# Projection's first product of blocks 2 to 28 made of seven 128x128 products, with half a tile lowered on VectorE and two row statistics on ScalarE

## The chip, the cores and the metric

The kernel runs on one core of a Trainium2 chip. The metric is the device time of one execution in microseconds. The kernel before took 998.61 us, the median of three runs (997.31 to 998.91).

Five engines work side by side, each through its own queue and in the order of that queue: TensorE (PE; its weight loads are shown apart as PEld), VectorE (DVE), ScalarE (ACT), GpSimd (POOL) and SyncE (SP), which issues the transfers. They wait for each other by semaphores.

## The reference

A cross attention with an adaptive layer norm in front and a residual behind, all in float32. With 16 sequences of 1024 rows (`x`) and of 64 context rows, width 512 and 16 heads of width 32:

```python
def _ada_ln(x, c, W_ss, b_ss):
    h = (x - mean(x)) / sqrt(var(x) + 1e-5)
    scale, bias = split(silu(c) @ W_ss + b_ss, 2)
    return (1 + scale)[:, None, :] * h + bias[:, None, :]

xq  = _ada_ln(x,   cond, Wss_q,  bss_q)        # (16, 1024, 512)
xkv = _ada_ln(ctx, cond, Wss_kv, bss_kv)       # (16,   64, 512)
q = (xq @ Wq + bq)                             # 16 heads of 32
k, v = split(xkv @ Wkv + bkv)
attn = softmax(q @ k.T / sqrt(32))             # over 64 context rows
return x + (attn @ v) @ Wp + bp
```

## The kernel before

The 16,384 rows of `x` are worked off in 32 blocks of 512 rows (`NB` = 32, `TB` = 512), four row tiles of 128 each. A block passes through: load, row statistics (`q_stats`, VectorE: L287 and L288 for each row tile; `q_scale` makes 1/sqrt(var) of them in small steps on ScalarE and GpSimd), normalising (`hidden`, ScalarE, L344), a transposition (`turn` on VectorE and `move` by transfers), scale and shift (`scale_features`, ScalarE, L459), the query product, the scores (`score_products`, L755, small tiles of 32x32), the softmax, the product with the values (`mix`, L1002 or L1013, small tiles), the projection, the addition of the residual (`added`, VectorE, L1288) and the store.

Softmax: the maximum over the context rows is taken on VectorE from PSUM (`maximum`, L772; `maxima`, L801 spreads it, tile `mb`), ScalarE copies the scores from PSUM to memory (`copied`, L781, half a tile each, 128x1024), GpSimd subtracts the maximum (`subtract`, L814, 128x2048; two tiles, `s_tiles[i, 0]` and `s_tiles[i, 1]`, for a block), ScalarE takes the exponential (`weights`, L836), GpSimd adds the two tiles up (`total`, L902).

Both large products of a block are 512x512x512, and both are made by Strassen's way: seven products of half the size instead of eight, with sums of features and of weights ahead and sums of results behind. They are numbered 1 to 7 and made in the order that buffers allow. One such product is four matmuls of 128x128 weights by 128x256 features, two records each in the trace. For the query product, L551 are the plain products, and products 1 and 7 are taken apart once more: `quarter_products` (L622) makes each of seven products of 128x128, the first four, then three. For this GpSimd prepares sums of features (`feature_quarters`, L598 to L600) in `t_quarters`, ScalarE copies two intermediate results there (`quarter_copies`, L633), and VectorE makes three additions (`quarter_adds`, L639 to L641). `feature_sums` (L510, GpSimd) are the sums of the outer level.

The projection's outer level is `product(i, n)` (L1155), with the attention's result `ot`, weights `w_p_sb` or their sums `WT`, and PSUM banks `pp`, two for a block. `row_sum` (L1120 to L1127, GpSimd) are its sums of rows; `biased` (L1099, ScalarE) seeds a bank with the bias, and `output_seed` (L1108) copies the result of product 1 into the second bank, where product 2 is added. Products 1, 6, 5 and 3 go to the one bank, 2, 7 and 4 to the other. In before all seven are plain.

What an engine does next is not decided by a scheduler: the calls stand in an order written out by hand, and each engine takes its instructions in that order. Blocks 0 to 2 and the last ones are written out call by call; a loop between them (`for i in range(3, NB - 2)`) works on several blocks in each turn: scores of block `i`, projection of blocks `i - 1` and `i - 2`, query product of block `i + 1`, normalising of blocks `i + 3` and `i + 4`. Several functions that the changed order calls stand in the file before as well and are not called there, or for a few blocks only: `q_stats_two`, `q_square_mean`, `lowered`, `subtract_half` and the `inner_...` functions.

Of the kernel before, what the change touches and what calls it, by code (L numbers as in the profile page):

```python
# [15 lines left out]
P = 128  # L16
# [4 lines left out]
def cross_attention_block(  # L21
# [1587 lines left out]
    load_residual(0)  # L1609
    feature_sums(2, nc.gpsimd, (3,))  # L1610
    subtract(1, zs=(0,))
    q_stats(5, (0,))
    subtract(1, zs=(1,))
    value_move('B', (3,))
    q_stats(5, (1,))
    query_product(2, 2)
    q_stats(5, (2,))
    scale_features(3, (0,))
    turn(4, (0,))
    scale_features(3, (3,))  # L1620
    context_product('B', 'v', 3)
    load_residual(1)
    query_out(2, 2)
    value_move('B', (2,))
    query_product(2, 6)
    context_out('B', 'v', 3)
    hidden(4, (1,))
    scale_features(3, (2,))
    weights(1, 0)
    query_product(2, 7)  # L1630
    spread_rows(0)
    divided(0)
    query_out(2, 6)
    value_move('B', (1,))
    query_product(2, 5)
    value_move('B', (0,))
    query_out(2, 7)
    query_product(2, 4)
    query_added(2, 5)
    query_product(2, 3)  # L1640
    feature_sums(3, nc.gpsimd, (0,))
    turn(4, (1,))
    row_sums(0, 0)
    weights(1, 1)
    total(1)
    swapped(1)
    biased(0, 2)
    query_added(2, 4)
    feature_sums(3, nc.gpsimd, (1,))
    query_out(2, 3)  # L1650
    q_stats(5, (3,))
    hidden(4, (3,))
    q_scale(5)
    turn(4, (2,))
    product(0, 1)
    added(0, 1)
# [402 lines left out]
```

## Time and profile before

| What | Value |
|---|---|
| median of three runs | 998.61 us (997.31 to 998.91) |
| profiled execution, its time | 996.79 us |
| profiled execution, its span | 994.9 us |
| granted TensorE clock | 1.00 |
| TensorE busy | 982.9 us, 99% |
| VectorE busy | 898.5 us, 90% |
| GpSimd busy | 893.0 us, 90% |
| ScalarE busy | 780.2 us, 78% |
| one turn of the loop | 28.52 us |

The span runs from the first to the last instruction of the profiled execution; its time has 1.9 us more around it. In rows of the groups, the first number behind the bar is the time that the group was busy, the second the mean of one instruction in ns; behind the second bar stands the idle time of the engine just before them. In rows of the timeline the first number is the start, the second the duration, and xN says how many records one row holds; what stands in brackets is a wait and what ended it.

### The profile page before, as it was taken

Reading aid. Unit: us, or ns where it says so; the run is one execution under the profiler, and the core shown is the slowest. Engines: PE = TensorE matmul, PEld = TensorE weight load, DVE = VectorE, ACT = ScalarE, POOL = GpSimd, SP = SyncE. Lnnn points to the kernel's source line nnn. Section 1 sums busy time; section 2 is a strip of 40 time slices with the busy share of each in tenths; the row PEclk is TensorE's granted clock in tenths of the full one; section 3 lists DMA queues with packets and bytes.
Section 4 is the critical chain, followed back from the end, with each engine's and each line's share of the span. In section 5 each row is a group of like instructions: output and inputs, shape, how many; then the busy total and the mean of one; then the engine's idle time right before and its main releaser. Section 6 shows DMA issues by size and latency. Waiting matters only on the chain.

```text
span 994.9 us, 20661 instructions
## 1 busy us (share of the span) xinstructions
PE 982.9 (99%) x7501; PEld 767.7 (77%) x7501; DVE 898.5 (90%) x1326; ACT 780.2 (78%) x1169; POOL 893.0 (90%) x695
## 2 busy tenths in 40 slices
PE   8999999999999999999999999999999999999997
PEld 7888777777777777777777778777787787777776
DVE  7687899999999999999999999999999999987995
ACT  3878868888888888888888888888888888876540
POOL 2687999999999999999999999999999999999861
PEclk9999999999999999999999999999999999999999
DMA  9765755555656555556655555565555556544323
GB/s 316 257 173 148 172 161 143 156 161 171 190 181 181 164 152 164 142 180 191 184 178 159 160 154 151 182 188 181 178 152 172 149 155 182 148 135 131 116 90 108
DMA packets 114885, 165.52 MB, mean 166 GB/s; under 512 B 34872, under 2 KB 46160, under 8 KB 112864
## 3 DMA queue, kind: packets, MB, share of 16 engines
q1 hardware_dynamic: 114400, 163.67, 55.2%
q8 instruction: 60, 0.98, 0.4%
q0 software_dynamic: 384, 0.54, 0.2%
q14 instruction: 41, 0.34, 0.1%
HBM read 79.21 MB, written 34.60 MB: 114 GB/s over the span
## 4 chain that ended last, share of the span: by engine, by line
PE 94%; POOL 1%; DMA 1%; SPq 1%; DVE 1%; issue 1%; DVEq 0%; ACT 0%; POOLq 0%
PE pp L1155 37%; PE pq L551 29%; PE pq L622 10%; PE ps L755 7%; PE po L1002 6%; PE pk_A L551 1%; PE pv_B L551 1%; PE pk_B L551 1%; PE pv_A L551 1%; DMA w_k_sb<-in_L_xcond_Wkv_dram 1%; PE pp_0b L1155 1%; POOL sum L902 0%; SPq L166 0%; SPq L143 0%; DVE m L772 0%
## 5 line engine op out<-in xcount | busy, mean ns | idle before, releaser
L814 POOL TENSOR_TENSOR s<-s,mb 128x2048 f32<-128x2048 f32 x63 | 286.1, 4563 | 16.5 <-DVE mb L801 9.2
L1155 PE MATMUL pp<-w_p_sb,ot 128*128 128x256 f32 x756 | 178.9, 380 | 0.2 <-DVE ot L981 0.2
L772 DVE TRANSPOSE_TENSOR_REDUCE m<-ps 128x32 f32<-128x1024 f32 x128 | 152.3, 1226 | 10.0 <-PE ps L755 9.7
L781 ACT COPY s<-ps 128x1024 f32<-128x1024 f32 x126 | 127.4, 1013 | 41.8 <-PE ps L755 36.9
L1155 PEld LDWEIGHTS pp<-w_p_sb,ot 128*128 128x128 f32 x756 | 141.2, 190 | 21.9 <-issue 1.9
L662 ACT ACTIVATE qt<-pq,bias_t 128x256 f32<-128x256 f32 x256 | 107.5, 474 | 52.9 <-PE pq L622 27.8
L902 POOL TENSOR_TENSOR sum<-s,p 128x2048 f32<-128x2048 f32 x30 | 136.4, 4547 | 1.6 <-ACT p L836 1.6
L1288 DVE TENSOR_TENSOR r<-pp,r 128x512 f32<-128x512 f32 x188 | 123.6, 669 | 14.2 <-ACT xt L459 6.8
L551 PE MATMUL pq<-xt,w_q_sums 128*128 128x256 f32 x512 | 123.8, 385 | 0.0
L1155 PE MATMUL pp<-WT,ot 128*128 128x256 f32 x508 | 122.0, 383 | 0.0
L551 PEld LDWEIGHTS pq<-xt,w_q_sums 128*128 128x128 f32 x512 | 95.2, 190 | 34.3 <-issue 22.6
L1155 PE MATMUL pp<-WT,s 128*128 128x256 f32 x504 | 119.6, 380 | 0.7 <-DVE r L1288 0.5
L861 ACT ACTIVATE s<-s 32x2048 f32<-32x2048 f32 x60 | 114.6, 1910 | 1.5
L1155 PEld LDWEIGHTS pp<-WT,ot 128*128 128x128 f32 x508 | 94.2, 190 | 17.8 <-issue 3.0
L1155 PEld LDWEIGHTS pp<-WT,s 128*128 128x128 f32 x504 | 91.5, 191 | 11.9 <-DVE r L1288 1.4
L344 ACT ACTIVATE x<-x,rstdq 128x512 f32<-128x512 f32 x128 | 94.8, 807 | 1.0 <-POOL rstdq L305 0.9
L459 ACT ACTIVATE xt<-xt,ss_q 128x512 f32<-128x512 f32 x124 | 93.9, 807 | 0.5 <-DMA xt<-ht 0.3
L981 DVE TENSOR_TENSOR ot<-po,vb 128x1024 f32<-128x1024 f32 x64 | 75.5, 1219 | 18.8 <-PE po L1002 17.4
L287 DVE BATCH_NORM_STATS2 bs<-x 128x6 f32<-128x512 f32 x128 | 85.3, 666 | 0.0
L510 POOL TENSOR_TENSOR xt_sums<-xt 128x512 f32<-128x512 f32 x64 | 81.2, 1268 | 1.4 <-ACT xt L459 0.9
L374 DVE STREAM_TRANSPOSE ht<-x 128x512 f32<-128x512 f32 x124 | 77.7, 679 | 4.3 <-ACT x L344 2.2
L907 DVE TRANSPOSE_TENSOR_REDUCE lt<-sum 128x64 f32<-128x2048 f32 x31 | 71.6, 2310 | 6.2 <-POOL sum L902 3.9
(221 smaller groups left out, 1957.6 us busy)
## 6 DMA issues: line engine op xcount, KB each, us to landing
x<-in_x_dram SPq DMA_DIRECT2D x32, 1024.0 KB, 5.4
r<-in_x_dram SPq DMA_DIRECT2D x32, 1024.0 KB, 5.7
out_dram<-r SPq DMA_DIRECT2D x62, 512.0 KB, 5.0
xt<-ht SPq DMA_DIRECT2D x488, 64.0 KB, 2.0
p<-s SPq DMA_DIRECT2D x60, 256.0 KB, 3.8
wss_kv<-in_L_xcond_Wss_kv_dram SPq DMA_DIRECT2D x4, 512.0 KB, 7.2
wss_q<-in_L_xcond_Wss_q_dram SPq DMA_DIRECT2D x4, 512.0 KB, 10.5
vr<-ltd SPq DMA_DIRECT2D x128, 8.0 KB, 1.8
```

Source lines behind the costliest of these rows:

```text
L344: nc.scalar.activation(dst, src, AF.Identity, bias=rstd[:, 1, j : j + 1], scale=rstd[:, 0, j : j + 1])
L459: nc.scalar.activation(xt[:, :, c, :], xt[:, :, c, :], AF.Identity, scale=ss["q"][:, c, b : b + 1], bias=ss["q"][:, NC + c, b : b + 1],)
L551: nc.tensor.matmul(out_, lhsT=lhsT, rhs=rhs, start=new and m == 0 and c == 0, stop=c == HC - 1, skip_group_check=True,)
L622: nc.tensor.matmul(qa["q", k][:, q * P : (q + 1) * P], lhsT=lhsT, rhs=rhs, start=first and q == 0, stop=True, skip_group_check=True,)
L662: nc.scalar.activation(dst, src, AF.Identity, bias=bq_t[:, o : o + 1])
L772: nc.vector.tensor_reduce(m_tiles[i][:, z, 2 * e : 2 * e + 2, :], s_banks[i, z][e].rearrange("p r (j a) -> p r j a", a=32), AX.X, ALU.max, ...
L781: nc.scalar.copy(s_tiles[i, z][:, 2 * e : 2 * e + 2, :], s_banks[i, z][e])
L814: eng.tensor_tensor(s_tiles[i, z], s_tiles[i, z], mb_tiles[i], ALU.subtract)
L861: nc.scalar.activation(s_tiles[i, 0][at + 32 : at + 64], raw_tiles[i][at : at + 32], AF.Exp, scale=SCALE)
L902: nc.gpsimd.tensor_tensor(t, s_tiles[i, 0], s_tiles[i, 1], ALU.add)
L1155: nc.tensor.matmul(to, lhsT=rows[:, c, t * P : (t + 1) * P], rhs=cols[:, c, :], start=n == 2 and (i, 2) not in seeded and t == 0 and c == ...
L1288: nc.vector.tensor_add(r, a, r)
```

## The change

Four things change together.

1. The projection's product 1 of blocks 2 to 28 is made of seven 128x128 products (`inner_products`, TensorE, L1246, four and then three), as products 1 and 7 of the query already are. With it come for each of these blocks: `inner_quarters` (GpSimd, L1223 to L1225), `inner_biased` (two ScalarE copies of 128x256, L1205 and L1206, instead of one of 128x512, L1099), `inner_copies` (ScalarE, L1257) and `inner_adds` (VectorE, L1263 to L1265). `inner_weight_sums(1)` (six sums on GpSimd, L1188 to L1195) runs once. One of its results is written over a 128x128 piece of `w_p_sb`, which is loaded again (64 KB) before the plain product 1 of block 30.
2. In these blocks one half of the second score tile is lowered by its maximum on VectorE straight from PSUM (`lowered(i, 0)`, L818) instead of being copied by ScalarE and lowered by GpSimd; GpSimd does the other half only (`subtract_half`, L825, 128x1024, instead of L814 with 128x2048).
3. The statistics of row tiles 0 and 1 of blocks 7 to 31 are made on ScalarE (`q_stats_two`: two activations with an accumulated output each, L331 and L332) with one small GpSimd instruction (`q_square_mean`, L337), instead of L287 and L288 on VectorE.
4. The order from `mix(0)` on is rewritten. In the turn of block `i` products 3 and 4 are now of block `i - 3` and the mix and the first products of block `i - 2`, so the projection lags further behind; the loop runs over 5 to 27, and blocks 28 to 31 are written out.

Instructions, before and after: L1155 884 to 776 matmuls of 128x256, L1246 0 to 189 of 128x128; L287 and L288 136 to 86 each; L818 2 to 29; L781 126 to 99; L814 63 to 36; L825 0 to 27.

The diff, cut to its core (in the loop the conditions that always hold are left out):

```diff
@@ load_projection
         if again:
-            nc.sync.dma_start(w_p_sb[:, : NC // 2, :], src[:, : NC // 2, :])
+            nc.sync.dma_start(w_p_sb[:, 0, P : 2 * P], src[:, 0, P : 2 * P])
@@ head, blocks 2 and 3
...
+    subtract(3, zs=(0,))
+    lowered(3, 0)
...
+    mix(2)
+    subtract_half(3, 1, 1)
...
+    inner_weight_sums(1)
+    query_product(4, 5)
+    feature_quarters(5, 1)
+    query_out(4, 7)
+    divided(2, (0,))
+    inner_quarters(2, 1)
+    turn(6, (3,))
+    inner_biased(2, 1)
+    q_stats_two(7, (0,))
+    q_stats_two(7, (1,))
...
@@ the loop
-    for i in range(3, NB - 2):
+    for i in range(5, NB - 4):
...
+            lowered(a, 0)
+            product(i - 3, 3)
+            product(i - 3, 4)
+            subtract(a, zs=(0,))
...
+            mix(b)
...
+            inner_biased(b, 1)
+            weights(a, 0)
+            quarter_products(i, 7, False)
+            subtract_half(a, 1, 1)
...
+            inner_quarters(b, 1)
+            query_out(i, 7)
+            total(a)
+            turn(f, (2,))
+            q_stats_two(i + 3, (0,))
+            inner_products(b, 1, True)
+            inner_copies(b, 1)
+            query_added(i, 5)
+            turn(f, (3,))
+            load_x(i + 4)
+            inner_adds(b, 1)
+            query_product(i, 4)
+            query_product(i, 3)
+            query_added(i, 4)
+            move(f, ks=(0,))
+            q_stats_two(i + 3, (1,))
+            row_sum(b, 0)
+            inner_products(b, 1, False)
...
+            output_seed(b)
...
@@ block 30, near the end
+    load_projection(again=True)
+    query_product(z, 3)
...
+    product(y - 1, 1)
```

The functions of the inner product, which both files hold:

```python
def inner_products(i, v, first):
    w, s = (lambda m, c: inner_weight(v, m, c)), (lambda k: inner_sum(v, k))
    t, x = inner_tiles[i, v], inner_rows(i, v)
    if first:
        todo = ((0, w(0, 0), x[:, 0, 0, :]), (2, s(0), t[:, 0]),
                (1, s(2), t[:, 1]), (3, s(1), t[:, 2]))
    else:
        todo = ((0, w(0, 1), x[:, 0, 1, :]), (2, s(3), x[:, 1, 1, :]), (1, w(1, 1), t[:, 3]))
    for q, rhs, lhsT in todo:
        nc.tensor.matmul(acc[acc_bank(i, v)][:, q * P : (q + 1) * P], lhsT=lhsT, rhs=rhs, ...)

def inner_adds(i, v):
    a, t, tt = acc[acc_bank(i, v)], inner_tiles[i, v], nc.vector.tensor_tensor
    both_ = a[:, P : 3 * P].rearrange("p (k n) -> p k n", k=2)
    tt(t[:, 2], a[:, 3 * P :], t[:, 0], ALU.add)
    tt(both_, both_, t[:, 2:3].to_broadcast([P, 2, P]), ALU.add)
    tt(a[:, 3 * P :], a[:, P : 2 * P], t[:, 1], ALU.add)
```

TensorE's queue in a turn of the loop, between the mix and the next scores. L551 and L622 are the query, `pp` the projection; in before:

```order
L551 MATMUL pq_1_3746<-xt_3385,w_q_sums 128x256 x4
L1155 MATMUL pp_2_3890<-w_p_sb,ot_3879 128x256 x4
L551 MATMUL pq_7_3816<-xt_sums,w_q_sb 128x256 x4
L1155 MATMUL pp_2_3904<-w_p_sb,ot_3879 128x256 x4
L551 MATMUL pq_1_3746<-xt_3385,w_q_sums 128x256 x4
L1155 MATMUL pp_3_3953<-WT,ot_3879 128x256 x4
```

The same place in after:

```order
L551 MATMUL pq_1_5498<-xt_5171,w_q_sums 128x256 x4
L1246 MATMUL pp_2_5676<-w_p_sb,ot_5697 128x128
L1246 MATMUL pp_2_5676<-first_sums,first_5701 128x128
L1246 MATMUL pp_2_5676<-w_p_sb,first_5701 128x128
L1246 MATMUL pp_2_5676<-first_sums,first_5701 128x128
L551 MATMUL pq_7_5628<-xt_sums,w_q_sb 128x256 x4
L551 MATMUL pq_1_5498<-xt_5171,w_q_sums 128x256 x4
L1246 MATMUL pp_2_5676<-w_p_sb,ot_5697 128x128
L1246 MATMUL pp_2_5676<-first_sums,ot_5697 128x128
L1246 MATMUL pp_2_5676<-w_p_sb,first_5701 128x128
```

The four matmuls of product 1 became seven small ones around two query products, and products 2 and 7 of the block moved behind the scores.

GpSimd's queue at the entry of the loop, behind the query's weight sums, in before (`s`, `mb`: scores and maxima; `t_quarters`, `xt_sums`: features of the query; L1120, L1122 and L1125: sums of rows for the projection):

```order
L814 TENSOR_TENSOR s_0_1584<-s_0_1584,mb_1641 128x2048
L814 TENSOR_TENSOR s_1_1617<-s_1_1617,mb_1641 128x2048
L1120 TENSOR_TENSOR s_2_1725<-ot_1719 128x512
L1122 TENSOR_TENSOR ot_1719<-ot_1719 128x2x256
L902 TENSOR_TENSOR sum_1755<-s_0_1584,p_1742 128x2048
L1125 TENSOR_TENSOR s_2_1774<-ot_1719,s_2_1725 128x512
```

And in after, for the same block's subtraction:

```order
L814 TENSOR_TENSOR s_0_1527<-s_0_1527,mb_1637 128x2048
L825 TENSOR_TENSOR s_1_1594<-s_1_1594,mb_1637 128x1024
L1188 TENSOR_TENSOR first_sums<-w_p_sb 128x128
L1189 TENSOR_TENSOR first_sums<-first_sums,w_p_sb 128x128
L1190 TENSOR_TENSOR w_p_sb<-w_p_sb 128x128
L1191 TENSOR_TENSOR first_sums<-w_p_sb,first_sums 128x128
L1194 COPY first_bias<-b_p_sb 128x128
L1195 TENSOR_TENSOR first_bias<-b_p_sb 128x128
L598 TENSOR_TENSOR t_quarters<-xt_1497 128x256
L599 TENSOR_TENSOR t_quarters<-xt_1497,t_quarters 128x128
L600 TENSOR_TENSOR t_quarters<-xt_1497,t_quarters 128x128
L1223 TENSOR_TENSOR first_1734<-ot_1732 128x256
```

The second subtraction is half as wide, the weight sums and the sums of both kinds stand ahead of the sums of rows and of the row total L902.

ScalarE's queue in the loop around the seed of product 1, in before (L836: exponentials, L662: the query's result, L459: scale and shift):

```order
L1099 COPY pp_2_6050<-b_p_sb 128x512
L836 ACTIVATE s_0_5904<-s_0_5904 128x2048
L836 ACTIVATE p_6062<-s_1_5937 128x2048
L1108 COPY pp_2_6064<-pp_2_6050 128x512
L459 ACTIVATE xt_5815<-xt_5815,ss_q 128x4x128 x3
L1099 COPY pp_3_6113<-b_diff 128x512
```

And in after:

```order
L1205 COPY pp_2_5676<-first_bias 128x256
L1206 COPY pp_2_5676<-zero 128x256
L836 ACTIVATE s_0_5497<-s_0_5497 128x2048
L836 ACTIVATE p_5691<-s_1_5586 128x2048
L662 ACTIVATE qt_5604<-pq_7_5628,bias_t 128x2x4x32 x2
L331 ACTIVATE squares_0_5711,mvq_5710<-x_5439 128x512
L332 ACTIVATE squares_0_5711,mvq_5710<-x_5439,mvq_5710 128x512
L1257 COPY first_5701<-pp_2_5676 128x256
L331 ACTIVATE squares_1_5742,mvq_5710<-x_5439 128x512
L332 ACTIVATE squares_1_5742,mvq_5710<-x_5439,mvq_5710 128x512
```

Between the exponentials and the seed of product 2 there now stand the query's result, four statistics and the inner copy, which TensorE's last three small matmuls need by way of VectorE.

More of the change, by code (lines that the diff above doesn't have):

```diff
@@ new lines, in cross_attention_block @@
+    added(1, 4)
+    inner_products(2, 1, True)
+    quarter_products(5, 1, True)
+    inner_copies(2, 1)
+    q_stats(7, (2,))
+    move(6, ks=(0,))
+    q_stats(7, (3,))
+    total(3)
+    move(6, ks=(1,))
+    quarter_copies(5, 1)
+    query_added(4, 4)
+    scale_features(5, (2,))
+    score_products(4, 0)
+    copied(4, 0, 1)
+    inner_adds(2, 1)
+    inner_products(2, 1, False)
+    output_seed(2)
+    row_sum(2, 2)
+    swapped(3)
+    quarter_adds(5, 1)
+    move(6, ks=(2,))
+    scale_features(5, (3,))
@@ L1787, in cross_attention_block @@
[L1787 to L1803 removed]
+        if i >= 4:
+            biased(b, 3)
@@ new lines, in cross_attention_block @@
+    subtract(27, zs=(0,))
+    lowered(27, 0)
+    quarter_products(28, 7, True)
+    turn(30, (0,))
+    query_out(28, 6)
+    scale_features(29, (0,))
+    product(25, 3)
+    scale_features(29, (1,))
+    quarter_copies(28, 7)
+    spread_rows(26)
+    product(25, 4)
+    quarter_adds(28, 7)
+    hidden(30, (2,))
+    mix(26)
+    turn(30, (1,))
+    added(25, 3)
+    scale_features(29, (3,))
+    subtract_half(27, 1, 1)
+    divided(26, (0,))
+    weights(27, 0)
+    quarter_products(28, 7, False)
@@ new lines, in cross_attention_block @@
+    divided(26, (1,))
+    feature_quarters(29, 1)
+    turn(30, (2,))
+    q_stats_two(31, (0,))
+    inner_biased(26, 1)
+    query_out(28, 7)
+    weights(27, 1)
+    turn(30, (3,))
+    query_product(28, 5)
+    inner_quarters(26, 1)
+    inner_products(26, 1, True)
+    query_product(28, 4)
+    added(25, 4)
+    query_added(28, 5)
+    inner_copies(26, 1)
+    query_product(28, 3)
+    inner_adds(26, 1)
+    inner_products(26, 1, False)
+    q_stats_two(31, (1,))
+    move(30, ks=(0,))
+    query_added(28, 4)
@@ new lines, in cross_attention_block @@
+    hidden(31, (3,))
+    turn(31, (0,))
+    added(26, 3)
+    scale_features(30, (2,))
+    query_out(29, 7)
+    row_sum(26, 3)
+    turn(31, (1,))
+    product(26, 4)
+    turn(31, (2,))
+    spread_rows(27)
+    mix(27)
+    query_added(29, 5)
+    query_product(29, 3)
+    load_residual(27)
+    inner_biased(27, 1)
+    divided(27, (0,))
+    subtract(28, zs=(0,))
+    turn(31, (3,))
+    added(26, 4)
+    subtract_half(28, 1, 1)
+    scale_features(30, (3,))
+    feature_sums(30, nc.gpsimd, (0,))
@@ new lines, in cross_attention_block @@
+    weights(28, 0)
+    move(31, ks=(0,))
+    move(31, ks=(1,))
+    move(31, ks=(2,))
+    query_product(29, 4)
+    feature_quarters(30, 1)
+    feature_sums(30, nc.gpsimd, (1,))
+    inner_quarters(27, 1)
+    weights(28, 1)
+    inner_products(27, 1, True)
+    query_out(29, 3)
+    divided(27, (1,))
+    total(28)
+    query_added(29, 4)
+    inner_copies(27, 1)
+    quarter_products(30, 1, True)
+    quarter_copies(30, 1)
+    inner_adds(27, 1)
+    swapped(28)
+    score_products(29, 0)
@@ new lines, in cross_attention_block @@
+    scale_features(31, (0,))
+    product(27, 4)
+    subtract(29, zs=(0,))
+    weights(29, 0)
+    added(27, 5)
+    product(27, 3)
+    lowered(29, 0)
+    load_residual(NB - 1)
+    spread_rows(28)
+    mix(28)
+    quarter_adds(30, 7)
+    added(27, 3)
+    divided(28, (0,))
+    quarter_products(30, 7, False)
+    subtract_half(29, 1, 1)
+    inner_quarters(28, 1)
+    query_product(30, 5)
+    inner_biased(28, 1)
+    query_out(30, 7)
+    added(27, 4)
+    weights(29, 1)
+    inner_products(28, 1, True)
```

829 lines of the change are left out of this document (543 added, 286 removed).

## The prediction

> **What bounds the kernel now.** I read the page first: busy shares, then the chain that ended last.
>
> ```profile
> span 994.9 us, 20661 instructions
> PE 982.9 (99%) x7501; PEld 767.7 (77%) x7501; DVE 898.5 (90%) x1326; ACT 780.2 (78%) x1169; POOL 893.0 (90%) x695
> PE 94%; POOL 1%; DMA 1%; SPq 1%; DVE 1%; issue 1%; DVEq 0%; ACT 0%; POOLq 0%
> ```
>
> TensorE is busy 982.9 of 994.9 us and the chain lies on it for 94%; VectorE and GpSimd follow at 90%. The waits of TensorE agree (total, times, longest): beside the start of the program none is above 0.6 us. Below them stands one of four windows, each one turn of the loop (28.52 us between equal instructions), and the mean of the four; the columns are PE, PEld, DVE, ACT, POOL.
>
> ```profile
> PE pc L210 <- DMA early<-in_cond_dram: 2.7, 1, 2.7
> PE ps L755 <- ACT qt L662: 0.6, 1, 0.6
> ```
>
> ```profile
> 478.25:506.77 28.52, 28.52 (x221) 22.20 (x220) 26.96 (x40) 24.02 (x36) 27.51 (x22) 1.00 0.57 170
> ...
> sum 114.08, PE 114.08 PEld 88.77 DVE 108.01 ACT 96.03 POOL 110.11; mean PE 28.52 PEld 22.19 DVE 27.00 ACT 24.01 POOL 27.53
> ```
>
> In the loop TensorE never idles, at granted clock 1.00. So only less TensorE work shortens a turn, and only while VectorE (27.00), GpSimd (27.53) and ScalarE (24.01) stay below the new period and hand over in time.
>
> **TensorE's part.** The timeline of TensorE gives the price of both kinds of product, start to start (x counts two records per matmul).
>
> ```profile
> 502.66 0.38 PE L622 MATMUL pq<-xt_sums,w_q_sums 128*128 128x128 f32 x2
> 502.88 0.83 PE L622 MATMUL pq<-t_quarters,w_p_sb 128*128 128x128 f32 x6
> 503.55 1.89 PE L1155 MATMUL pp<-w_p_sb,ot 128*128 128x256 f32 x8
> 505.28 1.89 PE L1155 MATMUL pp<-WT,ot 128*128 128x256 f32 x8
> ...
> 518.38 1.96 PE L1155 MATMUL pp<-WT,ot 128*128 128x256 f32 x8
> 520.26 1.14 PE L755 MATMUL ps<-qt,K_B 32*32 32x512 f32 x32
> 521.33 0.49 PE L622 MATMUL pq<-xt,w_q_sb 128*128 128x128 f32 x2
> ```
>
> A plain product (8 records 128x256) holds TensorE 505.28 − 503.55 = 1.73 us. Eight records 128x128 take 503.55 − 502.66 = 0.89, or 0.111 each; the nested product has seven matmuls, 14 records, 1.56. Saved: 0.165 per block, and for blocks 2 to 28, 27 of them, **4.5 us**. The new period would be 28.36. A change between full and small tiles costs about 0.15 (518.38 + 1.73 = 520.11, but the scores start at 520.26); the built program has 200 such changes in both kernels, so nothing is added there.
>
> The rows weigh against a rule of the Trainium skill ("TensorE: Matmul & The Clock Gate", section "Back-to-back issue gap"): in a stream of weight load and matmul pairs, spacing is set by both, about 81 ns a matmul at N=128 and 131 at N=512. By that rule halving N would not halve the time. It is rival D below; here 0.111 against 0.216 is a half.
>
> ```profile
> L622 PEld LDWEIGHTS pq<-t_quarters,w_q_sb 128*128 128x128 f32 x224 | 29.5, 192 | 0.0
> ```
>
> A weight load lasts 192 ns by its record, yet records follow each other every 111 ns, so loads overlap among themselves.
>
> **VectorE.** Rows from the groups of instructions.
>
> ```profile
> L818 DVE TENSOR_TENSOR s<-ps,mb 128x1024 f32<-128x1024 f32 x2 | 2.4, 1220 | 0.1
> L287 DVE BATCH_NORM_STATS2 bs<-x 128x6 f32<-128x512 f32 x128 | 85.3, 666 | 0.0
> L288 DVE BATCH_NORM_AGGREGATE mvq<-bs 128x2 f32<-128x6 f32 x128 | 23.3, 182 | 4.4
> L639 DVE TENSOR_TENSOR t_quarters<-pq,t_quarters 128x128 f32<-128x128 f32 x56 | 15.0, 267 | 2.1 <-ACT t_quarters L633 2.1
> L640 DVE TENSOR_TENSOR pq<-pq,t_quarters 128x256 f32<-128x256 f32 x56 | 24.2, 433 | 1.9
> L641 DVE TENSOR_TENSOR pq<-pq,t_quarters 128x128 f32<-128x128 f32 x56 | 16.8, 299 | 1.9
> ```
>
> Per turn it gains one `lowered` (1.22) and three inner additions of the shapes of L639 to L641 (0.27 + 0.43 + 0.30 = 1.00), and loses two statistics pairs (2 x 0.85 = 1.70): 27.00 + 0.52 = 27.5 of 28.36. Still covered, with 0.8 us to spare instead of 1.5.
>
> **ScalarE.**
>
> ```profile
> L781 ACT COPY s<-ps 128x1024 f32<-128x1024 f32 x126 | 127.4, 1013 | 41.8 <-PE ps L755 36.9 <-DVE m L772 3.9
> L344 ACT ACTIVATE x<-x,rstdq 128x512 f32<-128x512 f32 x128 | 94.8, 807 | 1.0 <-POOL rstdq L305 0.9
> L297 ACT ACTIVATE workq<-workq,ln_half 128x4 f32<-128x4 f32 x34 | 10.1, 297 | 1.1
> L1099 ACT COPY pp<-b_p_sb 128x512 f32<-128x512 f32 x31 | 18.4, 593 | 0.2 <-DVE r L1288 0.2
> L633 ACT COPY t_quarters<-pq 128x256 f32<-128x256 f32 x56 | 21.0, 374 | 2.7 <-PE pq L622 1.8
> ```
>
> It loses one copy (1.01) and gains an inner copy (0.37), two seed copies of 256 for one of 512 (2 x 0.37 − 0.59 = 0.15), and four statistics. No statistic with an accumulated output is in this trace. Lower end: a plain copy of 512 without one, 0.59. Upper end: L344 plus a whole small instruction for writing the accumulator, 0.81 + 0.30 = 1.11. I take 0.81, an activation of the same size from memory to memory. Sum: 24.01 − 1.01 + 0.37 + 0.15 + 3.24 = **26.8** (25.9 to 28.0), below 28.36 even at the upper end, but there with hardly any slack; it becomes the bound from 1.21 per statistic on.
>
> The Trainium skill ("ScalarE: Activation LUTs", section "What ACT_TABLE_LOAD costs") gives 186 ns plus 0.833 ns per element, and 93 more per pointer operand; from that an estimate is 0.61 for the mean and 0.71 for the square, which would make the sum 26.2. L344 has two such operands, where the page's estimate is 0.80 and the trace has 0.807.
>
> **GpSimd.** Its timeline in the first turns, start to start:
>
> ```profile
> 100.76 9.09 POOL L814 TENSOR_TENSOR s<-s,mb 128x2048 f32<-128x2048 f32 x2 [3.52 <-DVE mb L801]
> ...
> 186.90 0.74 POOL L598 TENSOR_TENSOR t_quarters<-xt_sums 128x256 f32<-128x256 f32 x1
> 187.72 0.46 POOL L599 TENSOR_TENSOR t_quarters<-xt_sums,t_quarters 128x128 f32<-128x128 f32 x1
> 188.26 0.45 POOL L600 TENSOR_TENSOR t_quarters<-xt_sums,t_quarters 128x128 f32<-128x128 f32 x1
> 188.67 9.08 POOL L814 TENSOR_TENSOR s<-s,mb 128x2048 f32<-128x2048 f32 x2
> 197.71 1.29 POOL L1120 TENSOR_TENSOR s<-ot 128x512 f32<-128x512 f32 x1
> 199.08 1.28 POOL L1122 TENSOR_TENSOR ot<-ot 128x512 f32<-128x512 f32 x1
> 200.61 4.54 POOL L902 TENSOR_TENSOR sum<-s,p 128x2048 f32<-128x2048 f32 x1 [0.25 <-ACT p L836]
> ...
> 217.15 9.08 POOL L814 TENSOR_TENSOR s<-s,mb 128x2048 f32<-128x2048 f32 x2
> ```
>
> From 188.67 to 217.15 are 28.48 us with one wait of 0.25: 28.2 of work per turn. A full subtraction costs (197.71 − 188.67)/2 = 4.52. Half of one is not in the trace: at the least a 128x512 one (1.28), at the most the full one (4.52); by the straight line through the two sizes 2.36, which I take. Three quarter sums take 188.67 − 186.90 = 1.77. The mean of squares is tiny, 0.1 to 0.45 (L600 is larger); I take 0.3. Sum: 28.2 − 4.52 + 2.36 + 1.77 + 0.3 = **28.1** of 28.36 (27.0 to 30.3). GpSimd stays as tight as before: 0.25 us of slack per turn.
>
> **The entry of the loop** is where that hurts. GpSimd works through from 100.76 on in before; the window that begins there says the same, 103.41 us of busy time in 105.84:
>
> ```profile
> 100.69:206.53 105.84, 105.56 (x761) 81.72 (x760) 95.60 (x137) 85.38 (x126) 103.41 (x72) 1.00 0.60 168
> ...
> 100.69 1.09 PE L1002 MATMUL po<-s,V_A 64*32 64x512 f32 x16
> ```
>
> The changed order starts from the same place (`mix(0)` on TensorE at 100.69, the subtraction of block 1 on GpSimd at 100.76). From there I counted each queue up to the first inner product of block 3, the second turn that has one. GpSimd, through the second of its three inner sums: nine full subtractions and row totals (40.7), two halves (4.7), 28 sums of 128x512 at 1.26 (35.3), three sets of small statistics (3.0), five sets of quarter sums (8.9), the quarter sums of query weights (1.8), the six new weight sums of 128x128 at about 0.45 (2.7), the inner sums (3.1) and one mean (0.3): 100.5, so ready at 201.2. TensorE up to there: 168 matmuls of 128x256 (72.6), 38 of 128x128 (8.5), 160 small ones of scores and mix (13.9), 19 tile changes (2.8): 97.8, so wanted at 198.5. TensorE comes early because the projection of older blocks has been pushed behind this point, and GpSimd comes late because of the weight sums. It has to stand still about **2.7 us** in blocks 1 to 3. With the half subtraction at its ends, this stall is 0.6 or 7.0. It is paid once: afterwards GpSimd (28.1) is the faster of the two.
>
> Other edits: the reload of a 64 KB piece of the weights is one more DMA on SP's queue, with the third query product and the scores of block 31 as cover (1.73 and about 1.07, from the starts above); 0.5 to 1 us of exposure if that cover is gone. In the tail TensorE waits 0.6 and less four times before; the new tail has three projection products less of the last block but one behind it and the same dependence on the row maxima, so I leave it at zero, plus or minus 0.5. For hand-overs inside the loop that are just missed I put 0.4 in all.
>
> **Sum**: −4.5 + 2.7 + 0.4 = −1.4 us of the 994.9 span, 993.5; the profiled execution was 996.79, the median of the runs 998.61, so I shift by 3.7 and get **997.2**.
>
> **Rivals.**
> A. The stall at the entry does not appear, since other engines let TensorE fall behind there anyway, or GpSimd's work fits its waits: then the whole saving stays, 998.6 − 4.4 = 994.2. For it: in before GpSimd is no less loaded and TensorE loses 0.28 of 105.84 there. Against: the count. Chance 0.23.
> B. Slower: the inner product's second half becomes a wait in every turn. TensorE issues four inner matmuls, two query products (3.46 us), and then three inner matmuls that need `inner_adds`; these stand in VectorE's queue behind a transposition and a query addition, and need `inner_copies`, which stands in ScalarE's queue behind the first two statistics. Worked out: up to 1.62 for the statistics already begun, 0.37 copy, 1.00 additions, about 0.7 for what VectorE has begun: 3.7 against 3.46. It decides from 0.05 us per turn on (27 x 0.05 = 1.4, the forecast gain). At 0.2 it costs 5.4, so 1002.6; at the upper price of a statistic (2.2 for the two) 0.8 a turn, 1019. For it: four engines at 95 to 99% of the period. Against: in before GpSimd at 28.2 of 28.52 costs nothing. Chance 0.20.
> C. The half subtraction costs nearly a full one: a stall of 7.0 at the entry, net +2.9, 1001.5, and GpSimd's 30.3 would then bound the loop, +1.9 x 25 more. For a price near the line speak both sizes. Chance 0.10, mostly near 1001.
> D. The 128-wide pieces pay for their weight loads: 14 x 0.192 = 2.69 against 1.73, +0.96 x 27 = 26 us, 1024. The starts of L622 speak against it. Chance 0.02.
>
> **Numbers.** The forecast (own range 995.5 to 998.9) has 0.45. A change of 0.2%, 2 us, is about what a measurement of this kernel tells from none. Faster: A, and a quarter of the forecast, 0.35. Slower: most of B, half of C, and D, 0.23. Same: the rest, 0.42. Range: A's 994.2 less 0.2 below; above up to B's first case, 1002.
>
> **What would show it.** Right: L1246 with 128x128 records 0.111 apart; a loop period of 28.36 with TensorE at 100%; waits of TensorE for GpSimd's `pp`, `s` or `first` in about 170 to 200 us, 2 to 3 us in all; L331 and L332 near 0.8; L825 near 2.36. Wrong: a period of 28.5 or more with waits on VectorE at L1246 (B), L825 near 4.5 (C), L1246 0.19 apart (D), or no waits before 210 us (A).

## The result, and the profile after

The changed kernel takes 1060.95 us (median of four runs, 1056.81 to 1062.59) against 998.35 for the kernel before (four runs of its own): a ratio of 1.062, with a 95% interval of 1.059 to 1.066. It is 62.6 us slower. Forecast were 997.2 us and a range of 994 to 1002. The profiled execution took 1056.81 us, its span is 1055.0, against 994.9.

The page of the changed kernel, its busy shares and its chain:

```profile
span 1055.0 us, 21526 instructions
PE 1003.3 (95%) x7663; PEld 783.9 (74%) x7663; DVE 914.0 (87%) x1334; ACT 834.3 (79%) x1396; POOL 885.8 (84%) x807
PE 45%; DMA 17%; DVE 14%; SPq 12%; issue 8%; POOL 2%; ACT 2%; DVEq 0%; POOLq 0%; ACTq 0%
PE pq L551 14%; PE pp L1155 13%; SPq L399 9%; DMA x<-in_x_dram 6%; DMA ltd<-lt 4%; DMA vr<-ltd 4%; PE ps L755 4%; DVE r L1288 4%; PE pq L622 3%; PE pp L1246 3%; DVE ot L981 3%; DVE ht L374 3%; SPq L927 2%; DVE m L772 1%; PE po L1002 1%
```

No engine took TensorE's place as the bound: PE has 95%, the others less. What came into the chain is SyncE's queue and transfers, 29% of the span together (DMA 17%, SPq 12%), where before had 2%. `L399` is `move`, `ltd` and `vr` are the row sums of the softmax on their way through memory (`inverse_rows`: one store, L925, and four loads, L927). One turn of the loop, columns as before (PE, PEld, DVE, ACT, POOL):

```profile
485.15:515.90 30.75, 29.27 (x228) 22.79 (x227) 27.41 (x40) 26.32 (x45) 27.14 (x26) 1.00 0.50 150
```

Waits by total, number and longest, of all engines and of SyncE's queue:

```profile
ACT pp L1205 <- DVE r L1288: 62.6, 24, 3.7
DVE vb L957 <- DMA vr<-ltd: 60.3, 25, 4.4
...
PE pq L622 <- DVE pq L641: 30.7, 20, 4.1
PE pp L1246 <- POOL first L1223: 3.6, 20, 0.2
```

```profile
SPq L399 <- PE pq L551: 43.9, 26, 2.4
...
SPq L399 <- DMA x<-in_x_dram: 38.0, 18, 5.1
```

VectorE stands 60.3 us, 2.4 in each of 25 blocks, ahead of `spread_rows` (L957), for the row sums. In its queue behind that stand an addition of the residual, for which ScalarE's seed of product 1 (L1205) waits, and the query's additions, for which TensorE waits. Where the row sums are, SyncE's timeline shows. One turn in before:

```profile
486.10 0.38 SPq L119 DMA_DIRECT2D x<-in_x_dram  x1
489.86 1.15 SPq L841 DMA_DIRECT2D p<-s  x2
491.10 9.01 SPq L399 DMA_DIRECT2D xt<-ht  x12
500.21 0.53 SPq L925 DMA_DIRECT2D ltd<-lt  x1
501.89 1.75 SPq L927 DMA_DIRECT2D vr<-ltd  x4
503.98 2.41 SPq L399 DMA_DIRECT2D xt<-ht  x4
```

And in after, with VectorE's wait for the row sums of the turn ahead and one piece of the chain of work:

```profile
515.88 0.38 SPq L119 DMA_DIRECT2D x<-in_x_dram  x1
517.92 2.44 SPq L399 DMA_DIRECT2D xt<-ht  x4
520.40 1.25 SPq L841 DMA_DIRECT2D p<-s  x2
521.69 12.62 SPq L399 DMA_DIRECT2D xt<-ht  x12
534.42 0.52 SPq L925 DMA_DIRECT2D ltd<-lt  x1
```

```profile
506.01 2.31 DVE L957 STREAM_TRANSPOSE vb<-vr 128x2048 f32<-128x2048 f32 x1 [2.53 <-DMA vr<-ltd]
...
524.64 0.51 DVE L922 RECIPROCAL lt<-lt 128x64 f32<-128x64 f32 x1
```

```profile
515.88 10.44 DMA x<-in_x_dram
...
526.33 0.51 SPq L399
```

The reciprocals of the row sums are done at 525.1, but their store is issued at 534.42, behind twelve `move`s. One of these waited until 526.33, when the 1 MB load of `x` had landed after 10.44 us. The program gives the transfers of a queue eight semaphores in turn, so that each waits for the one eight places ahead of it; the sixth `move` stands eight places behind the load, and both have the same semaphore in the trace. (The turn shown is the longest of the 23, 33.57 us; in the one ahead of it the twelve `move`s take 10.33.) In before, the twelve moves start 5.0 us behind the load, the row sums are issued 14.1 us behind it and not 18.5, and VectorE asks for them later.

From start to start of `spread_rows`, the loop takes (907.8 − 200.3)/23 = 30.76 us a turn, against (847.9 − 192.8)/23 = 28.48. Up to block 3's `spread_rows` the kernel is 7.5 us late (200.30 against 192.78), in the 23 turns behind it loses 52.4, and in the rest 0.2: 60.1, all of 1055.0 − 994.9.

### The profile page after: what moved, and what is told of

Same layout as the page of the kernel before. It is cut to its first block, busy times and chain, and to the rows that moved or that the text cites. A ratio compares the mean times of both kernels' runs of the same rounds, so it can differ in the third digit from the quotient of the medians.

```text
span 1055.0 us, 21526 instructions
## 1 busy us (share of the span) xinstructions
PE 1003.3 (95%) x7663; PEld 783.9 (74%) x7663; DVE 914.0 (87%) x1334; ACT 834.3 (79%) x1396; POOL 885.8 (84%) x807
## 4 chain that ended last, share of the span: by engine, by line
PE 45%; DMA 17%; DVE 14%; SPq 12%; issue 8%; POOL 2%; ACT 2%; DVEq 0%; POOLq 0%; ACTq 0%
PE pq L551 14%; PE pp L1155 13%; SPq L399 9%; DMA x<-in_x_dram 6%; DMA ltd<-lt 4%; DMA vr<-ltd 4%; PE ps L755 4%; DVE r L1288 4%; PE pq L622 3%; PE pp L1246 3%; DVE ot L981 3%; DVE ht L374 3%; SPq L927 2%; DVE m L772 1%; PE po L1002 1%
## 5 line engine op out<-in xcount | busy, mean ns | idle before, releaser
L814 POOL TENSOR_TENSOR s<-s,mb 128x2048 f32<-128x2048 f32 x36 | 163.8, 4554 | 11.4 <-DVE mb L801 7.5
L902 POOL TENSOR_TENSOR sum<-s,p 128x2048 f32<-128x2048 f32 x30 | 136.5, 4549 | 1.3 <-ACT p L836 1.3
L662 ACT ACTIVATE qt<-pq,bias_t 128x256 f32<-128x256 f32 x256 | 106.2, 466 | 35.6 <-PE pq L551 33.0
L1155 PE MATMUL pp<-w_p_sb,ot 128*128 128x256 f32 x540 | 127.9, 380 | 0.6 <-DVE ot L981 0.5
L551 PE MATMUL pq<-xt,w_q_sums 128*128 128x256 f32 x512 | 123.9, 386 | 2.6 <-ACT qt L662 1.8
L957 DVE STREAM_TRANSPOSE vb<-vr 128x2048 f32<-128x2048 f32 (+1 forms) x33 | 74.0, 2242 | 60.3 <-DMA vr<-ltd 60.3
L1155 PE MATMUL pp<-WT,ot 128*128 128x256 f32 x508 | 120.2, 380 | 0.5 <-ACT pp L1099 0.5
L1155 PE MATMUL pp<-WT,s 128*128 128x256 f32 x504 | 119.4, 379 | 1.1 <-DVE r L1288 1.1
L1155 PEld LDWEIGHTS pp<-w_p_sb,ot 128*128 128x128 f32 x540 | 100.0, 190 | 16.0 <-issue 1.7
L551 PEld LDWEIGHTS pq<-xt,w_q_sums 128*128 128x128 f32 x512 | 96.6, 194 | 17.6 <-DVE qt L669 3.2
L344 ACT ACTIVATE x<-x,rstdq 128x512 f32<-128x512 f32 x128 | 102.8, 814 | 5.4 <-POOL rstdq L305 4.4
L781 ACT COPY s<-ps 128x1024 f32<-128x1024 f32 x99 | 98.7, 999 | 10.6 <-PE ps L755 5.8
L1155 PEld LDWEIGHTS pp<-WT,s 128*128 128x128 f32 x504 | 95.4, 190 | 15.2 <-DVE r L1288 1.5
L1155 PEld LDWEIGHTS pp<-WT,ot 128*128 128x128 f32 x508 | 94.3, 190 | 13.4 <-ACT pp L1099 1.6
L459 ACT ACTIVATE xt<-xt,ss_q 128x512 f32<-128x512 f32 x124 | 97.2, 810 | 3.7 <-DMA ltd<-lt 2.4
L374 DVE STREAM_TRANSPOSE ht<-x 128x512 f32<-128x512 f32 x124 | 83.0, 689 | 6.2 <-ACT x L344 4.2
L551 PEld LDWEIGHTS pq<-xt,w_q_sb 128*128 128x128 f32 x288 | 52.2, 189 | 31.0 <-ACT pq L563 21.0
```

The lines of the kernel that those rows point to most:

```text
L344: nc.scalar.activation(dst, src, AF.Identity, bias=rstd[:, 1, j : j + 1], scale=rstd[:, 0, j : j + 1])
L374: nc.vector.transpose(ht_tiles[i][:, :, :, t, :].rearrange("p k c b -> p c k b"), x_tiles[i][:, t, :].rearrange("p (c k b) -> p c k b", c= ...
L551: nc.tensor.matmul(out_, lhsT=lhsT, rhs=rhs, start=new and m == 0 and c == 0, stop=c == HC - 1, skip_group_check=True,)
L662: nc.scalar.activation(dst, src, AF.Identity, bias=bq_t[:, o : o + 1])
L781: nc.scalar.copy(s_tiles[i, z][:, 2 * e : 2 * e + 2, :], s_banks[i, z][e])
L814: eng.tensor_tensor(s_tiles[i, z], s_tiles[i, z], mb_tiles[i], ALU.subtract)
```

## The experiments

Theory: SyncE's queue sets the turn, since the rewritten order puts large loads and sixteen moves between the row sums and the instruction that needs them. Rivals: the moves alone; the inner product's chain over ScalarE and VectorE (B of the prediction); engines too full. Each time is the median against 997 to 998 us for the kernel before on the same chip; turns are worked out as above.

**One load moved.** In the loop:

```diff
-            load_x(i + 4)          # ahead of move(f, ...)
...
             inverse_rows(a)
+            load_x(i + 4)
```

> The changed kernel with one move in the loop: load_x(i + 4), the 1 MB load of a block, stands behind inverse_rows(a) instead of ahead of the sixteen small transfers of move. Theory (the load holds SyncE's queue: the sixth move waits until the load has landed, 10.4 us, and the row sums' transfers behind it come late, so VectorE waits 2.4 us a turn at spread_rows): the wait of L957 for vr falls from 60 us to under 5, the turn from 30.75 to 28.4 to 28.7, and the time to 994 to 1004 us. Rival one (the twelve small moves themselves stand in the way, whatever the load does): the turn stays above 30, the time above 1040. Rival two (the inner product's chain over ScalarE and VectorE, rival B of the prediction, or engines too full): no change, 1055 to 1062.

Measured: 1038.41 us, ratio 1.041 (1.039 to 1.042), a turn of 30.0.

```profile
DVE vb L957 <- DMA vr<-ltd: 45.7, 25, 3.0
```

That is far above the theory's 994 to 1004. The load is a third of the loss, 22 us, and not the whole: the row sums still come 1.8 us late a turn.

**The row sums ahead of the twelve moves**, the load in its place:

```diff
             row_total(a)
+            inverse_rows(a)
...
-            inverse_rows(a)
```

> The changed kernel with another move: inverse_rows(a) directly behind row_total(a), so that its five transfers stand ahead of the twelve moves on SyncE; the load of x stays where it is. Theory (load of x): the second of these transfers is then the one that must wait for the load, lands at about 14 us behind the start of the load instead of 20, early enough for spread_rows; the turn falls to 28.4 to 29.3, the time to 995 to 1020, and moves now wait behind it. Rival one (the twelve moves): the turn falls to 28.4, 994 to 1003. Rival two (inner product's chain): no change, 1055 to 1062.

Measured: 1068.96, a miss for every theory as I had put it. VectorE hardly waits any more (4.8 us in all); the moves now come late, behind SyncE's own wait for the store to land, and ScalarE waits for the features:

```profile
ACT xt L459 <- DMA xt<-ht: 81.0, 23, 5.2
```

**Product 1 plain again**, in the changed order, with and without the load moved:

```diff
+    def inner_biased(i, v): biased(i, 2)
+    def inner_products(i, v, first):
+        if first: product(i, 1)
+    # inner_weight_sums, inner_quarters, inner_copies, inner_adds: nothing
```

> The changed kernel in its order, but product 1 of blocks 2 to 28 plain again (L1155, 128x256, seeded by one copy of 128x512), without the inner sums, copies and additions. Theory (the turn is set by transfers, not by engines): the time stays within 1050 to 1064 although TensorE has 4.5 us more work and VectorE and GpSimd have less. Rival two (the inner product's chain over ScalarE and VectorE sets the turn): 998 to 1006.

Measured: 1065.54, 4.6 us above the changed kernel and 1.5 above the expected band; the intervals of the two overlap.

> Both edits: product 1 plain, and the load of x behind inverse_rows. Against the kernel with the load moved alone it prices the nested product in a loop that TensorE bounds: theory (records of 128x128 0.111 us apart) 4.4 us more than that one, a turn of 28.52 and 998 to 1006 us. If both come out equal, something other than TensorE bounds the loop with the nested product, and its saving is lost there; if the plain one is faster, the nested product costs more than it saves.

Measured: 1038.42, equal to the run with the load moved (1038.41). There, 4.5 us of TensorE work more and 27 chains over ScalarE and VectorE less change nothing, and in neither pair does leaving out the inner product make the kernel faster. Rival B falls as the cause of the 62.6 us.

**Both moves; then the row sums taken apart** (store directly behind `row_total`, its four loads behind the next four moves):

```diff
             row_total(a)
+            inverse_store(a)
             ...
             move(f, ks=(1,))
+            inverse_load(a)
```

> Both earlier moves in one: the load of x late, and inverse_rows directly behind row_total, ahead of the twelve moves. Theory (a ring on SyncE: sixteen moves start when the query product 3 has freed their buffer, then the row sums' store and loads, then VectorE's spread_rows, then the attention's result, the inner product and the query products again; about 19 us of transfers and 12 of engines): the row sums no longer wait for the moves, VectorE's wait at spread_rows vanishes, and the turn is set by the moves landing in time for the features of the next turn, 28.4 to 29.3, time 996 to 1020. If a store on SyncE that waits holds the moves as in the second run, the time stays above 1035.

Measured: 1072.79, on the side of the expectation's second branch (above 1035); ScalarE waits 81.5 us for the features, as in the second run.

> The load of x late, and inverse_rows taken apart: its store directly behind row_total, its four loads behind the next four moves, so that SyncE does not stand in wait for the store to land. Theory of the ring: as the run before or 0.1 to 0.4 us a turn better, 995 to 1012. If the moves' place in the queue does not matter, as the run with the load late, 1038.

Measured: 1025.03 (1.027; 1.025 to 1.029), 13 us above its range. The only difference to the run before it is that four moves stand between the store and its loads, so that SyncE has work while the store lands: 48 us. SyncE's own wait for the store (L927, here L934), in the run before it and in this one:

```profile
SPq L927 <- DMA ltd<-lt: 72.6, 32, 4.6
```

```profile
SPq L934 <- DMA ltd<-lt: 14.4, 9, 4.2
```

**VectorE's order alone**, no transfer touched; then with the load moved:

```diff
-            spread_rows(b)
             added(i - 3, 3)
             ...
             added(i - 3, 4)
+            spread_rows(b)
```

> The changed kernel with no transfer moved: on VectorE alone spread_rows(b) stands behind added(i - 3, 3), quarter_adds(i, 7) and added(i - 3, 4) instead of ahead of them. 2.3 us of work then fill the wait for the row sums. Theory of the ring: the ring gets 2.3 us shorter (30.75 to 28.5), ScalarE's wait at the seed of product 1 falls from 63 us to under 15, time 998 to 1020. If it is not a ring but the transfers' own pace, the wait only moves and the time stays above 1050.

> spread_rows later on VectorE and the load of x late. Theory of the ring: the ring is then 3 us under what the engines need, TensorE bounds the turn at 28.36, time 994 to 1002, and what is left over against the kernel before are the entry of the loop and the tail.

Measured: 1032.62 and 1034.08, both above their ranges. The wait at L957 falls to 2.0 us in all and the one at L1205 to 1.5 (in the run without the load moved), and nearly every turn is 29.78, whether or not the load is moved. VectorE's detour moved the wait on: `ot` comes too late for the inner sums on GpSimd, and TensorE stands at the inner product (which it should reach at 502.38 + 1.73 = 504.11), in the run without the load moved:

```profile
502.38 1.89 PE L551 MATMUL pq<-xt,w_q_sums 128*128 128x256 f32 x8
504.59 0.46 PE L1246 MATMUL pp<-w_p_sb,ot 128*128 128x128 f32 x2 [0.33 <-ACT qt L662]
505.31 0.49 PE L1246 MATMUL pp<-first_sums,first 128*128 128x128 f32 x2 [0.26 <-POOL first L1223]
```

```profile
504.53 0.73 POOL L1223 TENSOR_TENSOR first<-ot 128x256 f32<-128x256 f32 x1 [1.39 <-DVE ot L981]
```

The row names ScalarE behind the first of TensorE's two waits, but what the instruction waits for is VectorE's semaphore; the first half of `ot` is done at 504.45.

**Both large loads behind the row sums**; then the loads ahead of the loop as well; then with product 1 plain:

```diff
-            load_residual(a)
-            load_x(i + 4)
             inverse_rows(a)
+            load_residual(a)
+            load_x(i + 4)
```

> The changed kernel with both 1 MB loads of the loop, load_residual(a) and load_x(i + 4), behind inverse_rows(a); VectorE's order as in the changed kernel. Theory (large loads ahead of small transfers on SyncE slow these and hold the queue, and the row sums come late): moves and row sums run at 0.6 us each, the row sums land about when spread_rows wants them, the turn falls from 30.75 to 28.4 to 29.0, time 1000 to 1018; 7.5 us of the loss, in blocks 0 to 3 ahead of the loop, stay. If the late load of x was all that the loads can do, 1038 as that run.

> As the run before, and ahead of the loop too: load_x(6) behind the transfers of swapped(1), load_residual(1) behind the sixteen moves of block 4, load_x(7), load_residual(2) and load_x(8), load_residual(3) behind the row sums of their places. Theory: ScalarE's wait of 5.0 us for p at 126 us goes, with TensorE's 2 us behind it; 3 to 6 us less than the run before, 996 to 1013. GpSimd (the prediction's term) would be unmoved by this: no difference.

> The same with product 1 plain. If TensorE bounds the loop in the run before, this one is 3 to 5 us slower; if other waits still do, equal within 2 us.

Measured: 1040.85, 1040.87 and 1043.94. All three are misses of the theory's numbers: without any large load ahead of the moves the row sums still come late (38.0 us in the first). The moves start only when the query's product 3 has freed the feature buffer, and they and the row sums are about 18 us of issue (510.06 to 527.98 in one turn of the first), with the landing to come. In the first, the 23 turns take 5.7 us less than with the load of `x` alone moved, but the part behind them 6.0 more. Plain costs 3.1 us here, with intervals that overlap, so this run decides nothing. Ahead of the loop nothing was won in the median: VectorE's statistics of block 6 now wait 4.4 us for their load (3.5 in the changed kernel), and TensorE 4.25 behind them. No difference is also what the prediction's term would give, but TensorE's waits for GpSimd there are 0.2 us in all.

**The other direction: the kernel before, with one load moved.**

```diff
-            load_x(i + 5)
             swapped(i)
             query_product(n, 3)
+            load_x(i + 5)
             move(i + 3, ks=(0,))
```

> The kernel before, with one load moved: load_x(i + 5) directly ahead of the moves of block i + 3, behind swapped(i), instead of ahead of it; nothing else. Theory: the load then has only about 5 us less time ahead of the ninth transfer behind it, which waits for it; row sums come 2 to 4 us later, and there they have 0.5 us to spare: 1030 to 1090. If the queue has slack in before, 997 to 1000.

Measured: 1060.28 us, ratio 1.063 (1.060 to 1.065), a turn of 31.1. The new waits at L399 and L957 are those of the changed kernel, and a third, for the features at L459, comes with them; before has one of 1.5 us for `x` at L399, 1.1 us in all at L957 and 0.3 at L459. (What waits for the load is the eighth transfer behind it, not the ninth.)

```profile
SPq L399 <- DMA x<-in_x_dram: 57.6, 25, 3.3
```

```profile
DVE vb L957 <- DMA vr<-ltd: 65.4, 25, 5.6
ACT xt L459 <- DMA xt<-ht: 61.1, 23, 5.3
```

No arithmetic, no engine's order and no byte differs from the kernel before, only one transfer's place in SyncE's queue, and it costs 63 us. That a large load close ahead of the moves can make a loss of the whole size is shown.

**Further orders of the transfers** (on the kernel with all loads late): the last four moves behind the row sums; then the query's products 3 and 4 exchanged, to free the buffer earlier; then the statistics of block 6 later ahead of the loop; then that with product 1 plain.

```diff
-            move(f, ks=(3,))
             inverse_rows(a)
+            move(f, ks=(3,))
@@ second
-            query_product(i, 4)
             query_product(i, 3)
+            query_product(i, 4)
@@ third, ahead of the loop
-    q_stats(6, (0,)) ... q_stats(6, (2,))
     added(0, 6)
+    q_stats(6, (0,)) ... q_stats(6, (2,))
```

> The kernel with all large loads late, and the last four of the sixteen moves behind the row sums' transfers, as the kernel before has them. Theory of the ring (moves wait for the buffer that the query's product 3 frees; the row sums stand behind them): the row sums land 2.4 us earlier, VectorE's wait of 35 us at spread_rows falls under 10, the last moves come later by about 4 and ScalarE may wait up to 1 us a turn for them; a turn of 28.5 to 29.2, 1010 to 1030. If the engines' own work sets the turn of 29.6: no change, 1040.

> As the run before, and the query's products 3 and 4 change places, so that the feature buffer is free 1.73 us earlier and the moves start by so much earlier. Theory of the ring: neither the row sums nor the last moves are waited for, the turn falls to 28.4 to 28.8, 1000 to 1018. If the ring is not what is left: no change against the run before.

> As the run before, and ahead of the loop VectorE's statistics of block 6 stand behind the addition added(0, 6), so that VectorE does not stand 4.4 us in wait for the load of block 6. Theory (the 7.5 us lost ahead of the loop are waits for transfers passed on through VectorE's and ScalarE's queues): TensorE's wait of 4.25 us at 137 us goes, 3 to 5 us less, 996 to 1014. If GpSimd is what holds the head (the prediction), it then shows as waits for GpSimd and gives back 2.7 of it.

> As the run before with product 1 plain. In a loop that TensorE bounds it is 3 to 5 us slower than the run before (4.5 by the prediction's term). Equal within 1.5: the loop is still not TensorE's. Faster: the inner product's own chain is then the bound.

Measured: 1046.78, 1054.26, 1054.40 and 1055.53. The first three are misses; the last is equal to the one before it within the 1.5 us that stood for a loop that is still not TensorE's. In the first ScalarE waits for the features (46.7 us); in the other three VectorE's query addition waits for the product that now comes last (53.1 us in the second), and the turn is 30.55:

```profile
ACT xt L459 <- DMA xt<-ht: 46.7, 21, 3.4
```

```profile
DVE qt L669 <- PE pq L551: 53.1, 26, 2.2
```

Each order meets one deadline by missing another. The best one, the row sums taken apart with both loads behind:

> The best order so far (row sums' store directly behind row_total, its loads behind the second four moves, load of x behind both) with the residual's 1 MB load behind the load of x as well, so that it does not run beside the first moves. Theory (SyncE's queue from the free feature buffer to the next features is too long for the turn): the first four moves take 2.4 us instead of 3.5, the others 0.6 each, ScalarE's wait for the features falls from 1.5 to 2.2 us a turn to under 0.8; 1000 to 1018. If the large loads do not slow the small ones: 1025 as that run.

Measured: 1023.13 (1.026; 1.024 to 1.028), five us above its range; the features are still waited for, 32.4 us.

**Fewer issues, the same bytes.** On the kernel with both loads late, 1040.85 us:

```diff
         for k in ks:
+            nc.sync.dma_start(xt[32 * k : 32 * k + 32],
+                ht[0:32, k].rearrange(...).unsqueeze(1).to_broadcast([32, 4, NC, NT * 32]))
-            for g in range(4):
-                nc.sync.dma_start(xt[32 * k : 32 * k + 32, g], ht[32 * g : 32 * g + 32, k]...)
```

> The kernel with both loads late in the loop (1041 us), and in the loop each quarter of move is one transfer of 256 KB instead of four of 64 KB: the same bytes, 4 issues instead of 16. It reads the rows of one partition group four times, so the features of three groups are not the right ones. Theory (the number of issues on SyncE, 0.6 us each, makes the row sums and features late): both come 5 us or more earlier, VectorE's wait at spread_rows is gone, the turn is TensorE's own, 28.4 to 28.8, time 998 to 1012. If the bytes or the engines' own chains set the turn of 29.6: 1030 to 1041.

Measured: 1007.57 us (1.0096; 1.0081 to 1.0111), 33 us less than with sixteen issues (26.6 of it in the 23 turns) and in the expected range. It leaves three of the four feature groups out, so it is a test and no kernel to use. Nearly every turn is 28.60 us, and TensorE does not idle:

```profile
513.60:542.20 28.60, 28.60 (x228) 22.59 (x227) 27.33 (x40) 26.24 (x45) 27.08 (x26) 1.00 0.59 168
```

So the engines' own work is not what holds the changed order at 29.8 to 30.8 us a turn: it is the number of transfers that one queue has to issue between two deadlines. Whether their issue time counts more, or the waits for the transfer eight places ahead, which fall away with them, this run does not separate. With that out of the way the rest of the change can be read, in TensorE's timeline of the same run:

```profile
521.41 0.38 PE L1252 MATMUL pp<-w_p_sb,ot 128*128 128x128 f32 x2
...
522.30 1.89 PE L557 MATMUL pq<-xt_sums,w_q_sb 128*128 128x256 f32 x8
...
526.20 0.39 PE L1252 MATMUL pp<-w_p_sb,first 128*128 128x128 f32 x2
526.52 1.45 PE L761 MATMUL ps<-qt,K_B 32*32 32x512 f32 x32
527.90 0.49 PE L628 MATMUL pq<-xt,w_q_sb 128*128 128x128 f32 x2
```

```profile
526.85 0.21 PEld L761 LDWEIGHTS ps<-qt,K_B 32*32 32x32 f32 x24 [0.18 <-ACT qt L668]
```

(Lines are six higher in this file.) Four inner matmuls take 522.30 − 521.41 = 0.89 us, as forecast. The scores behind the inner product take 1.38, and 1.07 in before (520.26 to 521.33): they wait for the query's last result, behind which only three small matmuls stand now, where before had a whole product (0.18 of the wait shows at their weight loads). That costs 0.31 where 0.17 were saved, so the turn is 28.60 and not 28.36, and no better than before's 28.52.

## Why the prediction was wrong

**The step that failed** is the list of "other edits". It counted one transfer, the reload of 64 KB, gave all hand-overs inside the loop 0.4 us, and the prediction added up the work of TensorE, VectorE, ScalarE and GpSimd, but did not walk SyncE's queue. The moved steps issue 23 small transfers, two stores and two 1 MB loads a turn, and the rewritten order puts `move` and the loads at other distances from `inverse_rows` and `spread_rows`. The rows that would have told it stood in the trace of before: the last of the four loads of the row sums is issued at 503.21 (four loads from 501.89 to 503.64), lands 1.8 us behind that, at 505.0, and is needed at 505.68:

```profile
505.68 2.30 DVE L957 STREAM_TRANSPOSE vb<-vr 128x2048 f32<-128x2048 f32 x1
```

That is 0.7 us to spare. The missing term measured 52.4 us in the loop: there VectorE waits for row sums that SyncE issues late. It was in no rival, so the range could not hold it.

**The entry of the loop** was priced at 2.7 us by GpSimd's queue; 7.5 us were lost, hardly any of it in direct waits for GpSimd. The 1 MB loads stand ahead of `p` there, and ScalarE, with the query's results behind it, waits for `p`:

```profile
118.59 0.41 SPq L126 DMA_DIRECT2D r<-in_x_dram  x1
119.11 0.44 SPq L119 DMA_DIRECT2D x<-in_x_dram  x1
120.23 1.15 SPq L841 DMA_DIRECT2D p<-s  x2
```

```profile
130.99 1.91 ACT L861 ACTIVATE s<-s 32x2048 f32<-32x2048 f32 x1 [5.03 <-DMA p<-s]
```

```profile
133.80 1.99 PE L551 MATMUL pq<-xt,w_q_sums 128*128 128x256 f32 x8 [1.81 <-ACT qt L662]
136.93 1.99 PE L1155 MATMUL pp<-WT,s 128*128 128x256 f32 x8 [1.14 <-DVE r L1288]
149.62 1.80 PE L755 MATMUL ps<-qt,K_A 32*32 32x512 f32 x32 [1.72 <-ACT qt L662]
```

TensorE's waits for GpSimd's `first` are 0.2 us at most. The count of GpSimd's work was right: from 101.45 through the second inner sum of block 3 (207.85) it has 6.3 us of waits and 100.1 of work, against 100.5 counted. But those waits, for VectorE and ScalarE, were not in the count, and TensorE lost 6.5 us there in direct waits for the same two engines. So the stall that the sum priced did not come on top, as rival A had it, and the saving was lost all the same. How the 7.5 us divide is open: of the two attempts ahead of the loop one brings block 3 1.6 us forward in its trace (199.04 against 200.60) and the other does not, and neither shortens the median.

**Rival B** (a wait for the inner additions) is not the cause: without the inner product the kernel is no faster. A smaller relative of it did show up once the transfers were out of the way, the scores that wait for the query, 0.31 us a turn; B named another place.

**Right were the prices of single instructions.** The nested product is 1.56 us (0.89 + 0.67), which saves 0.17 a block; the prediction's sum has 0.165. Half a subtraction is 2.39 against 2.36, and a statistic 0.72 to 0.75 from start to start against 0.81:

```profile
L825 POOL TENSOR_TENSOR s<-s,mb 128x1024 f32<-128x1024 f32 x27 | 64.6, 2391 | 1.5 <-ACT s L781 1.5
L331 ACT ACTIVATE squares<-x 128x512 f32<-128x512 f32 x50 | 31.3, 626 | 0.0
L331 ACT ACTIVATION_READ_ACCUMULATOR squares<-x 128x1 f32 x50 | 9.6, 192 | 0.0
L332 ACT ACTIVATE squares<-x,mvq 128x512 f32<-128x512 f32 x50 | 36.1, 722 | 1.6
```

The estimates from the Trainium skill ("ScalarE: Activation LUTs", section "What ACT_TABLE_LOAD costs"), 0.61 and 0.71, fit the two activations, 0.626 and 0.722; the reading of the accumulator, an instruction of 0.19 us of its own, comes behind each and overlaps both neighbours in part.

The sums of the engines held too: in the last run's turn VectorE is busy 27.33 us (forecast 27.5), ScalarE 26.24 (26.8), GpSimd 27.08, against 28.1 that counted its small gaps as work. The rule of the Trainium skill that I had made rival D ("TensorE: Matmul & The Clock Gate", section "Back-to-back issue gap") does not show here: 0.111 us a record at 128 columns is half of 0.216 at 256.

**With the fewer transfers** the change still lost. Of the 10.7 us by which the last run's span (1005.6) exceeds before's, 6.6 are lost up to block 3 (199.4 against 192.8), 2.9 in the 23 turns, and 1.2 behind them. What is left open: whether an order exists that meets all deadlines with sixteen moves; none of those tried is faster than 1023 us in the median, and no version here beats the kernel before. All of them kept the moves in SyncE's queue. A rival way was not tried: `move` can give every second transfer to GpSimd's queue (`two=True`), as both kernels do for eight transfers of block 1. There such a transfer takes 0.52 us of GpSimd's time in the median; an estimate from that is 4.1 us for eight in a turn, more than the 1.5 us that GpSimd (27.08 of 28.60) has left.

## What to carry to other kernels

Walk the queue that issues the transfers like an engine: every transfer has an issue time (0.6 us for a `move` here), a deadline and a predecessor that it waits for, and a kernel whose engines are all at 95% or less was bound by it here. Before a step is moved, look up how much slack the transfers around it have in the trace of before: the gap between landing and first use, not the busy share. A waiting transfer at the head of a queue holds everything behind it; put short waits behind work that can be issued meanwhile (48 us between two orders that differ in that alone).

## What was not expected of the hardware

The 1 MB load of `x` lands after 5.4 us in the median of before, after 9.1 in the run of before with that load directly ahead of the moves, and after 8.0 in after; the residual's, of the same size, after 5.7 in before and 5.4 in after. `p` (256 KB) goes from 3.8 in before to 5.1 in after. Four transfers of 64 KB cost 4 x 0.6 us of issue, one of the same 256 KB costs 0.6, and lands after 5.1 us where a single 64 KB one takes 2.0. The granted clock, 1.000 in before, was 0.997 in the profile of after and 0.987 in that of the run with one load moved in before. It does not follow the waits alone: two executions with the row sums ahead of the moves had 1.000 at 1067 and 1068 us. What lowers it is not shown.
